# A decoder layer on one core: attention scores as one float32r product of high and low parts, strips spread in one transfer per half, maxima split and used on the chip

## The chip, the cores and the metric

The kernel runs on one core of a Trainium2 chip. The core has five engines with instruction streams of their own: TensorE (PE, with its weight loads shown as PEld), VectorE (DVE), ScalarE (ACT), GpSimd (POOL) and SyncE (SP), which here issues every DMA. The metric is the time of one execution on the device in microseconds, the median of the runs.

## What is computed

The reference is one decoder layer on 32 batches of 256 positions with 256 features. Three parts follow each other, each with a residual and a layer norm: a selective scan (state space) block, a cross attention with 16 heads of width 16, and a gated feed-forward net with 8 experts. The part that the change touches is the attention, shown here without the projections of q, k and v:

```python
scores = jnp.einsum('bhqd,bhkd->bhqk', q, k) / np.sqrt(D_K)   # 16 heads, D_K = 16
attn = jax.nn.softmax(scores, axis=-1)
out = jnp.einsum('bhqk,bhkd->bhqd', attn, v)
x = _layernorm(x + (out.transpose(0, 2, 1, 3).reshape(B, S, D_MODEL) @ w_o.T + b_o))
# before it: the scan block; after it: 8 experts, each on its own 32 positions
h_t = dA_t * h_{t-1} + dBu_t ;  y_t = sum_n h_t * C_t          # the scan, 512 x 16 states
out = (silu(x @ w1[e]) * (x @ w3[e])) @ w2[e]                  # an expert unit
```

## The kernel before

**Order of the work.** The kernel is a set of generators, each a chain of steps: `decays`, `scan`, `weighted`, `sums` for the scan block, `pres` and `steps` for its projections, `keys_ahead`, `keys`, `queries`, `maxima`, `attns`, `finishes` for the attention, `units` and `seconds` for the expert units. When the program is built, `in_order` picks the next step by a planned clock for each engine: `spend` adds a planned cost (`MM`, `EV`, `VE`, `CV`, `GP`, `LANDING`) and a chain says when its next step can start. So the instructions of an engine stand in one fixed order, written when the program is built, and each engine runs its own list in that order. A step that waits holds everything behind it in the same list. All DMAs stand in the list of SP.

**The scan.** There are 32 x 16 = 512 scan steps. A step loads a strip `ld` (two DMAs of 256 KB, `load_step`, three steps ahead), ACT makes `da` (L573), DVE multiplies `bu` (L602) and scans `h` (L621), POOL multiplies `h` by `c_bc` (L637), and after four steps TensorE sums `y` (L651). There are six `h` buffers.

**The attention before.** `keys_ahead` makes k for every batch, feature by position: a float32 product (L349), an ACT copy with the bias into `k_flat`, one DMA into `k_all` in the device's memory. `queries` does the same with q, into `heads`. `spread_heads` (L678) then reads them back so that each head has 16 of the 64 rows of a strip: for each half (8 heads) two DMAs for `kT` and two for `qT`. `qT` waits for `scored` of the batch before, which still uses the strip.

`scores` (L809) multiplies two heads at a time, one in rows 0 to 63 and one in rows 64 to 127 of the array, each in two tiles of 128 positions: four float32 products of 64 (or 63) x 128 by 64 x 256. `maxima` (L825) calls it with q on the left, 4 times for each half, and DVE takes the maximum over the keys (L838). TensorE transposes the maxima (L844), ACT negates them into `rows` (L847), one DMA writes them to the device's memory (`tops`) and another reads them back into row 63 of each strip of `qT`. Row 63 of `kT` holds ones there, so that `attns` (L874), which calls `scores` with k on the left and all 64 rows, gets scores with the maxima already subtracted. ACT takes the exponential (L894), TensorE multiplies by v (L863), and `finish` transposes, divides, projects (`ps_o`) and stores x2d.

**The experts.** 32 expert units need the x2d of eight batches each, or of four for the last eight units. The last four need batch 31. A unit loads weights and inputs, has products `ps_h` (L1133) for w1 and w3 and `ps_down` (L1212) for w2.

**PSUM.** The two-dimensional products share a ring of five banks (`ps_mm`), which `take` and `done` hand out.

Of the kernel before, what the change touches and what calls it, by code (L numbers as in the profile page):

```python
# [7 lines left out]

F32 = mybir.dt.float32
AF = mybir.ActivationFunctionType  # L10
ALU = mybir.AluOpType
AX = mybir.AxisListType
# [3 lines left out]
P = 128  # L16
B, L, D = 32, 256, 256
# [5 lines left out]
NQ = NS // NL  # L23
GB = 2
# [73 lines left out]
def decoder_kernel(ctx: ExitStack, tc: tile.TileContext, a: dict, out: bass.AP):  # L98
# [18 lines left out]

    k_all = dram.tile([B, D, L], F32, name="k_all")
    v_all = dram.tile([B, L, D], F32, name="v_all")
# [45 lines left out]

    def heads(n):

        w = wp.tile([P, 2, D], F32, tag="w_" + n, name="w_" + n)
        src = a["w_" + n].rearrange("(k p) (h c) -> p k h c", p=P, c=32)
        for k in range(2):  # L170
            dst = w[:, k].rearrange("p (h c) -> p h c", c=DK)
            dma(dst, src[:, k, :, :DK])
        bias = wp.tile([P, 2], F32, name="b_" + n)
        for g in range(NG):
            r = 64 * (g % 2)
            src = a["b_" + n].rearrange("(j c) g -> j c g", c=32)[:, :DK, g : g + 1]
            dma(bias[r : r + 64, g // 2 : g // 2 + 1], src)
        return w, bias
# [29 lines left out]

    later = []
    now, dma = dma, lambda dst, src: later.append((dst, src))  # L210
    w_k, b_k = heads("k")
    w_v = weight("w_v", D, D)
    b_out = row("b_out")
    w_out = weight("w_out", DI, D)
    w_q, b_q = heads("q")
    w_o = weight("w_o", D, D)
# [53 lines left out]

    kT = keep.tile([P, HG, L], F32, name="kT")
    last = small.tile([P, 1], F32, tag="ln_st", name="last")
    at = ident.rearrange("p (j c) -> p j c", c=HR)[:, :, HR - 1]
    nc.vector.tensor_reduce(last, at, AX.X, ALU.add)
    nc.vector.tensor_copy(kT.rearrange("p g t -> p (g t)"), last.to_broadcast([P, HG * L]))
    qT = keep.tile([P, HG, L], F32, name="qT")
    nc.gpsimd.memset(qT, 0.0)

# [27 lines left out]

    MM = 0.47
    EV = {1: 0.47, 2: 0.6, 4: 1.06}
    VE = {1: 0.41, 2: 0.69, 4: 1.23}
    CV = 0.565  # L310
    GP = {1: 0.7, 2: 1.27, 4: 2.36}

    def layernorm(tiles, t):

        n = len(tiles)
        mv = small.tile([P, n, 2], F32, tag="ln_mv", name="ln_mv")
        for i, x in enumerate(tiles):
            st = small.tile([P, 6], F32, tag="ln_st", name="ln_st")
            nc.vector.bn_stats(st, x)
            nc.vector.bn_aggr(mv[:, i, :], st)  # L320
        yield spend("DVE", 0.6 * n, t), "POOL"
        rstd = small.tile([P, n, 1], F32, tag="ln_rstd", name="ln_rstd")
        nc.gpsimd.tensor_scalar_add(rstd, mv[:, :, 1:2], EPS)  # L323
        nc.gpsimd.tensor_tensor(rstd, rstd, power[:, :n, :], ALU.pow)
        off = small.tile([P, n, 1], F32, tag="ln_off", name="ln_off")
        nc.gpsimd.tensor_tensor(off, mv[:, :, 0:1], rstd, ALU.mult)
        nc.gpsimd.tensor_scalar_mul(off, off, -1.0)
        yield spend("POOL", 1.5), "ACT"
        for i, x in enumerate(tiles):
            nc.scalar.activation(  # L330
                x, x, AF.Identity, bias=off[:, i, :], scale=rstd[:, i, :]
            )
        return spend("ACT", 0.6 * n)

# [29 lines left out]
    def rest():  # L364

        while later:
            yield 0.0, "SP"
            dma(*later.pop(0))

    xps, dds, sress, bcds, ygs, us, spread, silus = {}, {}, {}, {}, {}, {}, {}, []  # L370
# [175 lines left out]
    def decays():  # L546
# [15 lines left out]
        for i in range(STEPS):  # L562
# [8 lines left out]
            for g in range(GB):  # L571
                for q in range(NQ):
# [5 lines left out]
                    )  # L578
            decayed[i] = spend("ACT", GB * NQ * 0.5)

    read = {-1: 0.0}

    def scan():
# [4 lines left out]
        for i in range(STEPS):  # L588
# [39 lines left out]
            )  # L628
            recurred[i] = spend("DVE", 2.29)
            read[i] = max(multiplied, decayed[i])  # L630
# [45 lines left out]
    scored = {}  # L676

    def spread_heads(b, dst, d, t, there):  # L678

        yield t, "SP"  # L680
        for half in range(2):
            if b:
                yield lambda: max(t, scored[b - 1, half]) if (b - 1, half) in scored else None, "SP"
            for j in range(2):
                src = d.rearrange("(i g j c) t -> i j c g t", i=2, j=2, c=DK)[half, j]
                dma(dst[HR * j : HR * j + DK, 4 * half : 4 * half + 4, :], src)
            there[b, half] = clock.at["SP"] + LANDING
# [3 lines left out]
    def keys_ahead():  # L691

        for b in range(B):
# [14 lines left out]
            done(1, tk)  # L708
            yield tk, "SP"
            dma(k_all[b].rearrange("(m p) t -> p m t", p=P), flat)  # L710
            yield from take(1, rank, t0)
# [77 lines left out]
    def queries():  # L789
        for b in range(B):  # L790
# [12 lines left out]
            done(1, tq)  # L803
            yield tq, "SP"
            d = bcd.tile([D, L], F32, tag="heads", name="heads")
            dma(d.rearrange("(m p) t -> p m t", p=P), flat)
            yield from spread_heads(b, qT, d, clock.at["SP"] + LANDING, qts)

    def scores(heads, left, right, n):  # L809


        ss = [bank("s").rearrange("p (t n) -> p t n", t=2) for _ in heads]
        for t in range(2):
            for h, s in zip(heads, ss):
                g, r = h // 2, HR * (h % 2)
                nc.tensor.matmul(  # L816
                    s[:, t, :],
                    left[r : r + n, g, t * P : (t + 1) * P],
                    right[r : r + n, g, :],
                    start=True,  # L820
                    stop=True,
                )
        return ss, spend("PE", 2 * MM + 0.2)

    def maxima():  # L825

        for i in range(2 * B):
# [5 lines left out]
            while h < 8:  # L833
                yield from take(2, 2, t0)
                ss, ts = scores(range(8 * half + h, 8 * half + h + 2), qT, kT, HR - 1)
                for s in ss:
# [3 lines left out]
                    done(1, t)  # L840
                    h += 1
            yield from take(1, 1, t)
            ps = bank("ps_m")[:H, :P]
            nc.tensor.transpose(ps, top.rearrange("p j g t -> p (j g t)"), ident)  # L844
            yield spend("PE", 0.2), "ACT"
            rows = unit2.tile([H, P], F32, tag="rows", name="rows")
            nc.scalar.activation(rows, ps, AF.Identity, scale=-1.0)  # L847
            t = spend("ACT", 0.35)
            done(1, t)
            yield t, "SP"  # L850
            d = bcd.tile([2, 4 * L], F32, tag="tops", name="tops")
            dma(d.rearrange("j (i n) -> (j i) n", n=P), rows)
            yield clock.at["SP"] + LANDING, "SP"
            dst = qT[HR - 1 :: HR, 4 * half : 4 * half + 4]
            dma(dst.rearrange("j g t -> j (g t)"), d)
            tts[b, half] = clock.at["SP"] + LANDING

# [16 lines left out]
    def attns():  # L874

        for n in range(2 * B):
# [4 lines left out]
            for g in range(3):  # L881
                ess = []
                while g < 2 and len(ess) < 4:
                    yield from take(2, 2, tq)
                    h = 8 * half + 4 * g + len(ess)
                    ss, ts = scores(range(h, h + 2), kT, qT, HR)
                    if g and not ess:
# [454 lines left out]
```

## Time and profile before

| | |
|---|---|
| median of 3 runs | 2742.55 us (2738.98 to 2750.74) |
| profiled execution | 2743.78 us, span 2742.0 us |
| PE busy | 2466.3 us, 90% of the span |
| DVE busy | 2380.6 us, 87% |
| ACT busy | 2043.4 us, 75% |
| POOL busy | 1643.7 us, 60% |
| granted TensorE clock, mean | 0.959 |
| DMA | 505.86 MB, the main queue 64.8% of 16 engines |

The span runs from the first to the last instruction. Busy time is the union of an engine's instructions. A float32 product appears as two records, so 1024 products of `scores` for the maxima are 2048 records. The profile's slices show DVE at nine tenths or more until the last tenth of the span, where it falls to one to two tenths and TensorE goes on.

### The profile page before, as it was taken

How to read it: one execution, taken by the hardware profiler on the slowest of the kernel's cores; microseconds unless marked ns; L12 is line 12 of the kernel's file. 1: busy time of each engine (PE TensorE's matmuls, PEld its weight loads, DVE VectorE, ACT ScalarE, POOL GpSimd, SP SyncE). 2: the span in 40 equal slices, each digit the busy share in tenths (PEclk: the TensorE clock that was granted, in tenths of full speed). 3: DMA queues.
4: the chain of work that ended last, by engine and by line, in shares of the span. 5: the costliest groups of instructions: out<-in, count | busy, mean ns of one | idle time of the engine just before them, and what ended most of it. 6: DMA issues, size and time to landing. Idle time of an engine off the chain costs nothing.

```text
span 2742.0 us, 48659 instructions
## 1 busy us (share of the span) xinstructions
PE 2466.3 (90%) x16964; PEld 1705.3 (62%) x16964; DVE 2380.6 (87%) x2413; ACT 2043.4 (75%) x4327; POOL 1643.7 (60%) x1145
## 2 busy tenths in 40 slices
PE   5788989889899899989998989999999899998988
PEld 4565666566566666666666666665666566666767
DVE  4999999999999999999999999999999899896212
ACT  6887888888778878887878778888788788674331
POOL 4775766666666666575666665666666666553000
PEclk8899999999999999998999999999999999999999
DMA  7866666666676666676666666667666566666464
GB/s 203 228 199 176 193 187 181 189 191 191 187 199 186 181 167 190 176 197 177 167 198 187 198 175 186 187 177 195 190 197 179 163 172 180 185 174 181 150 195 144
DMA packets 491497, 505.86 MB, mean 184 GB/s; under 512 B 177204, under 2 KB 339252, under 8 KB 491252
## 3 DMA queue, kind: packets, MB, share of 16 engines
q1 hardware_dynamic: 491252, 502.75, 64.8%
q8 instruction: 135, 2.21, 0.4%
q14 instruction: 110, 0.90, 0.1%
HBM read 426.07 MB, written 76.55 MB: 183 GB/s over the span
## 4 chain that ended last, share of the span: by engine, by line
PE 29%; DVE 11%; ACT 8%; DMA 5%; issue 3%; POOL 1%; SPq 1%; DVEq 0%; ACTq 0%; POOLq 0%
PE ps_h L1133 8%; PE s L816 6%; DVE h L621 5%; PE ps_down L1212 4%; ACT da L573 3%; PE y L651 3%; DVE bu L602 2%; DVE tops L838 2%; PE ps_in L349 2%; PE ps_oT L863 2%; DMA ld<-dd 1%; DMA xe<-x2d 1%; PE ps_out L349 1%; PE ps_qk L349 1%; ACT es L894 1%
## 5 line engine op out<-in xcount | busy, mean ns | idle before, releaser
L637 POOL TENSOR_TENSOR h<-h,c_bc 128x1024 f32<-128x1024 f32 x512 | 1209.1, 2362 | 740.6 <-DVE h L621 627.0
L621 DVE TENSOR_TENSOR_SCAN h<-da,bu 128x1024 f32<-128x1024 f32 x512 | 1168.9, 2283 | 50.4 <-ACT da L573 5.8
L573 ACT ACTIVATE da<-ld,a_neg 128x252 f32<-128x252 f32 x2048 | 864.6, 504 | 188.3 <-DVE h L621 138.4
L602 DVE TENSOR_TENSOR bu<-ld,b_bc 128x1024 f32<-128x1024 f32 x512 | 626.1, 1223 | 19.9 <-DMA ld<-dd 8.0
L816 PE MATMUL s<-kT,qT 63*128 63x256 f32 x2048 | 345.4, 416 | 45.6 <-DVE tops L838 22.8
L894 ACT ACTIVATE es<-s 128x512 f32<-128x512 f32 x512 | 277.9, 594 | 140.6 <-PE s L816 75.9
L838 DVE TENSOR_REDUCE tops<-s 128x2 f32<-128x512 f32 x512 | 325.2, 677 | 41.6 <-PE s L816 41.1
L1133 PE MATMUL ps_h<-x2T,w 128*128 128x256 f32 (+2 forms) x1536 | 343.5, 368 | 9.5 <-ACT es L894 1.7
L816 PE MATMUL s<-qT,kT 64*128 64x256 f32 x2048 | 313.8, 405 | 22.5 <-DMA qT<-tops 13.0
L651 PE MATMUL y<-h,sel_y 128*32 128x256 f32 x4096 | 280.8, 397 | 52.3 <-POOL h L637 36.9
L816 PEld LDWEIGHTS s<-kT,qT 63*128 63x128 f32 x2048 | 213.8, 193 | 151.9 <-DVE tops L838 50.8
L1133 PEld LDWEIGHTS ps_h<-x2T,w 128*128 128x128 f32 (+1 forms) x1536 | 246.7, 186 | 89.7 <-issue 35.1
L349 PE MATMUL ps_in<-xT,w_in 128*128 128x256 f32 x1024 | 258.4, 397 | 8.7 <-ACT da L573 2.6
L816 PEld LDWEIGHTS s<-qT,kT 64*128 64x128 f32 x2048 | 200.9, 189 | 102.3 <-issue 39.6
L651 PEld LDWEIGHTS y<-h,sel_y 128*32 128x32 f32 x4096 | 131.8, 113 | 177.4 <-POOL h L637 55.1
L349 PEld LDWEIGHTS ps_in<-xT,w_in 128*128 128x128 f32 x1024 | 192.8, 196 | 60.4 <-issue 12.9
L420 POOL TENSOR_TENSOR u<-u,shifted 128x512 f32<-128x512 f32 x128 | 151.4, 1183 | 39.7 <-ACT u L407 34.7
L323 POOL TENSOR_SCALAR ln_rstd<-ln_mv 128x2 f32<-128x2 f32 x96 | 20.9, 218 | 254.2 <-DVE ln_mv L320 250.0
L407 ACT ACTIVATE shifted<-ps_in,tap_b,conv_w 128x256 f32<-128x256 f32 x256 | 130.8, 567 | 22.5 <-PE ps_in L349 10.9
L863 PE MATMUL ps_oT<-es,v 128*32 128x256 f32 x2048 | 142.4, 391 | 3.7 <-DVE h L1197 1.2
L349 PE MATMUL ps_out<-w_out,yg 128*128 128x256 f32 x512 | 117.6, 383 | 0.4 <-DVE yg L667 0.4
L375 ACT ACT_TABLE_LOAD x90 | 115.5, 1283 | 1.4
(135 smaller groups left out, 2987.5 us busy)
## 6 DMA issues: line engine op xcount, KB each, us to landing
ld<-dd SPq DMA_DIRECT2D x1024, 256.0 KB
w<-in_w SPq DMA_DIRECT2D x128, 352.0 KB
x<-in_x SPq DMA_DIRECT2D x64, 256.0 KB
dd<-delta SPq DMA_DIRECT2D x32, 512.0 KB
dd<-u SPq DMA_DIRECT2D x32, 512.0 KB
w<-in_w SPq DMA_DIRECT2D x32, 384.0 KB
w13y<-in_w SPq DMA_DIRECT2D x32, 352.0 KB
c_bc<-bcd SPq DMA_DIRECT2D x64, 128.0 KB
```

Of the source, the lines that this page charges most:

```text
L349: nc.tensor.matmul(ps[:, j, :], l, r, start=(k == 0), stop=(k == len(terms) - 1))
L420: nc.gpsimd.tensor_tensor(u[:, cc], u[:, cc], at, ALU.add)
L573: nc.scalar.activation(da[:, g, q].rearrange("p (k t) -> p k t", t=CHUNK)[:, :, 1:], loads[i][:, 0, g].rearrange("p (k t) -> p k t", t=CHU ...
L602: nc.vector.tensor_tensor(bu, loads[i][:, 1].unsqueeze(2).to_broadcast([P, GB, NQ, L]), b_bc.unsqueeze(1).to_broadcast([P, GB, NQ, L]), AL ...
L621: nc.vector.tensor_tensor_scan(h.rearrange("p g q t -> p (g q t)"), das_of.pop(i).rearrange("p g q t -> p (g q t)"), bu.rearrange("p g q t ...
L637: nc.gpsimd.tensor_tensor(hs[i], hs[i], c_bc, ALU.mult)
L651: nc.tensor.matmul(y[32 * j : 32 * j + 32, :], sel_y[:, g, :], hs[i - NJ + 1 + j][:, g, q, :], start=(g == 0 and q == 0), stop=(g == GB - ...
L816: nc.tensor.matmul(s[:, t, :], left[r : r + n, g, t * P : (t + 1) * P], right[r : r + n, g, :], start=True, stop=True,)
L838: nc.vector.tensor_reduce(top[:, h % 2, h // 2, :], s, AX.X, ALU.max)
L863: nc.tensor.matmul(oT[32 * j : 32 * j + 32, :], v[:, k, 4 * g + j, :], ess[j][:, k, :], start=(k == 0), stop=(k == 1), tile_position=(0, 3 ...
L894: nc.scalar.activation(es, s, AF.Exp, scale=1.0 / DK**0.5)
L1133: nc.tensor.matmul(ps[:m, i, :], w_tiles[u, which, e][k][:, f * P : f * P + m], right, start=(k == 0), stop=(k == 1),)
```

## The change

- **High and low parts.** After the bias, POOL copies q or k to a float32r tile (`hi`), and subtracts it from the full value into `lo`, which takes the place of the flat tile. `k_all` gets three parts (hi, lo, hi), `heads` gets two (hi, lo). The features are ordered by column position first, so that one half of the heads lies in one block of 128 rows. The weights `w_k` and `w_q` are reordered once by POOL at the start, and their biases come in eight small DMAs each instead of four.
- **Strips.** All 64 rows of a strip are filled by one transfer of 64 rows x 4 KB instead of 16 rows of 4 x 1 KB: In blocks of 16 rows `kT` holds hi, lo, lo, hi and `qT` holds hi, lo, hi, lo. One float32r product over 64 rows then adds all four products of the parts.
- **Scores.** `scores` uses float32r operands and all 64 rows. For `attns` each product is followed by a second one, `pick` (a column with ones at the head's two rows, high and low, spread over 128 columns) times `mTs`, which adds the negated maximum in the same PSUM bank.
- **Maxima.** POOL splits the maxima of a half into `padded` (high, low), TensorE transposes two blocks of 128x128, ACT negates them into `mTs`. The two DMAs through `tops`, and row 63 as a place for them, are gone.
- **Planned costs.** Several constants of the planner are different (`MM`, `EV`, `VE`, `CV`, `GP`, the costs of `decays`, `scan`, `layernorm`), so every list is ordered anew.

```diff
+    def parts_of(n, b, full, t, d):
+        hi = unit1.tile([P, 2, L], F32R, tag="hi", name=f"{n}_hi_{b}")
+        lo = full.bitcast(F32R)
+        yield t, "POOL"
+        nc.gpsimd.tensor_copy(hi, full)
+        nc.gpsimd.tensor_tensor(lo, full, hi.bitcast(F32), ALU.subtract)
+        t = spend("POOL", 2 * GP[2])
+        yield t, "SP"
+        for s, part in enumerate((hi, lo, hi)[: d.shape[1]]):
+            dma(d[:, s].rearrange("i p t -> p i t"), part.bitcast(F32))
...
     def spread_heads(b, dst, d, t, there):
...
             for j in range(2):
-                src = d.rearrange("(i g j c) t -> i j c g t", i=2, j=2, c=DK)[half, j]
-                dma(dst[HR * j : HR * j + DK, 4 * half : 4 * half + 4, :], src)
+                at = dst[HR * j : HR * (j + 1), NG * half : NG * (half + 1), :]
+                at = at.bitcast(F32).rearrange("p g t -> p (g t)")
+                src = d[half, 0, NG * j : NG * (j + 1)]
+                again = 0 if dst is qT else P * L
+                rows = [[again, 2], [2 * NG * L, 2 * DK], [1, NG * L]]
+                dma(at, bass.AP(src.tensor, src.offset, rows))
...
-            yield tk, "SP"
-            dma(k_all[b].rearrange("(m p) t -> p m t", p=P), flat)
+            yield from parts_of("k", b, flat, tk, k_all[b])
...
-            yield tq, "SP"
-            d = bcd.tile([D, L], F32, tag="heads", name="heads")
-            dma(d.rearrange("(m p) t -> p m t", p=P), flat)
+            d = bcd.tile([2, 2, P, L], F32, tag="heads", name="heads")
+            yield from parts_of("q", b, flat, tq, d)
...
-    def scores(heads, left, right, n):
+    def scores(heads, left, right, lowered):
...
-                    left[r : r + n, g, t * P : (t + 1) * P],
-                    right[r : r + n, g, :],
+                    left[r : r + HR, g, t * P : (t + 1) * P],
+                    right[r : r + HR, g, :],
                     start=True,
-                    stop=True,
+                    stop=not lowered,
                 )
+            for h, s in zip(heads, ss):
+                g, r = h // 2, HR * (h % 2)
+                if lowered:
+                    nc.tensor.matmul(
+                        s[:, t, :],
+                        pick[r : r + HR, g : g + 1].to_broadcast([HR, P]),
+                        mTs[g // NG][r : r + HR, :],
+                        start=False,
+                        stop=True,
+                    )
...
+            yield t, "POOL"
+            r = 2 * NG * half
+            hi, lo = padded[:, :, :, r : r + NG], padded[:, :, :, r + NG : r + 2 * NG]
+            full = top.rearrange("p j g t -> p t j g")
+            nc.gpsimd.tensor_copy(hi, full)
+            nc.gpsimd.tensor_tensor(lo, full, hi.bitcast(F32), ALU.subtract)
+            t = spend("POOL", 0.5)
             yield from take(1, 1, t)
-            ps = bank("ps_m")[:H, :P]
-            nc.tensor.transpose(ps, top.rearrange("p j g t -> p (j g t)"), ident)
-            yield spend("PE", 0.2), "ACT"
-            rows = unit2.tile([H, P], F32, tag="rows", name="rows")
-            nc.scalar.activation(rows, ps, AF.Identity, scale=-1.0)
...
-            dma(d.rearrange("j (i n) -> (j i) n", n=P), rows)
-            yield clock.at["SP"] + LANDING, "SP"
-            dst = qT[HR - 1 :: HR, 4 * half : 4 * half + 4]
-            dma(dst.rearrange("j g t -> j (g t)"), d)
+            ps = bank("ps_m")[:, :L]
+            for k in range(2):
+                src = padded[:, k].rearrange("p j r -> p (j r)").bitcast(F32)
+                nc.tensor.transpose(ps[:, k * P : (k + 1) * P], src, ident)
+            yield spend("PE", 0.6), "ACT"
+            nc.scalar.activation(mTs[half], ps, AF.Identity, scale=-1.0)
```

## The prediction

> **What bounds the kernel now.** I read the page first: VectorE is busy 87% of the span and TensorE 90%, but not in the same places. So the second view is a table of stretches, cut where the last of the 512 scan steps ends (2513.4 us). Columns: stretch, its length, then busy time with instructions of PE, PEld, DVE, ACT, POOL, then granted clock, DMA share, GB/s.
>
> ```profile
> 0.00:2513.40 2513.40, 2268.35 (x15567) 1545.11 (x15567) 2327.76 (x2294) 1972.37 (x4194) 1623.93 (x1095) 0.96 0.66 186
> 2513.40:2742.00 228.60, 198.00 (x1399) 160.22 (x1397) 52.85 (x119) 71.03 (x133) 19.76 (x50) 0.93 0.54 172
> ```
>
> Two stages, two limits. Up to the last scan DVE works 2327.8 of 2513.4 us; 37 us of its idle time lie in the first 60 us. The tail of 228.6 us is TensorE's. So the change can gain in the first stage only what DVE loses to others, and in the tail whatever it takes from TensorE's list. Third view, who made DVE wait between 60 and 2513 us (total, times, longest):
>
> ```profile
> DVE tops L838 <- PE s L816: 22.5, 26, 3.5
> DVE yg L667 <- PE y L651: 16.1, 14, 3.0
> DVE xe L1224 <- PE ps_down L1212: 13.0, 4, 6.9
> DVE x L964 <- PE ps_o L349: 10.2, 9, 2.6
> ```
>
> All rows of that answer with PE as releaser add up to 78 us, those with ACT, POOL or DMA to about 10; the other 60 us of idle time are short gaps between neighbours (bu ends, the scan starts 0.13 us later). So 78 us is what a faster TensorE can give back there.
>
> **Scores on TensorE.** Fourth view, the timeline of PE, start and length of merged pieces; the distance between two starts is the price.
>
> ```profile
> 1016.63 1.14 PE L816 MATMUL s<-qT,kT 64*128 64x256 f32 x8
> 1017.70 0.66 PE L935 MATMUL ps_oB<-ident,oS 128*128 128x128 f32 x4
> ...
> 1031.06 1.05 PE L863 MATMUL ps_oT<-es,v 128*32 128x256 f32 x16
> 1032.03 1.99 PE L1133 MATMUL ps_h<-x2T,w 128*128 128x256 f32 x8
> ```
>
> One call of scores() is four float32 products, shown as 8 records, and takes 1.07 us: 133 ns a record. 512 calls take 548 us (the groups show 659 busy, since ends overlap waits). No float32r product is in this trace. Upper bound: it costs what a float32 one does, two records, 265 ns. Lower bound: the cheapest 256-column record of the trace, 61 ns (0.97 us for the 16 of ps_oT, four side by side). I take one record instead of two, 133 ns, the row of the same shape and row groups. A call for maxima keeps four products: 0.53 us. A call for attention gets four more, pick times mTs: 1.06 us, no gain. Sum 256 x (0.53 + 1.06) = 407 us, so 141 us less; with 61 ns 187 us, 361 us less; with 265 ns 814 us, 266 us more. The transpose of the maxima becomes two products of 128x128 (the 4 of ps_oB take 0.53 us, so 0.13 each): 64 x 0.13 = 8 us more.
>
> The Trainium skill (TensorE: Matmul & The Clock Gate, sections "Back-to-back issue gap" and "LDWEIGHTS") gives N/2.4 + 2.5 ns for a pass, 109 ns at 256 columns, and P/1.2 for a weight load whatever the rows, 107 ns at 128 columns. That speaks against the pick products, which load 128 columns of weights to subtract one row of maxima: by it a call is bound by its loads, 0.43 us for maxima and 0.85 us for attention, and the sum would be 328 us. The load records of L816 here last 182 to 190 ns, longer than the page's 107, but most lie beside a product.
>
> **What of that reaches the scan.** I price each product in PE's instruction list (256 columns 0.456 us, 128 columns 0.237, ps_oT 0.122, y 0.111, transposes 0.135, scores as above). Up to the last y product the old list holds 2086 us of work in 2518 us, the new one 1995. TensorE isn't full there; it is late at single moments, in order, behind other products. With a shorter list I let half of the 78 us go: -39 us. Both ends stay: 0 and -78.
>
> **DVE** has the same 2413 instructions. In its new order 24 expert units end before the last scan instead of 23 (4.3 us each), and the last two reductions of batch 30 stand before it: +6 us before the last scan.
>
> **POOL** gets, for k and for q of each batch, a copy and a subtraction of 128x512. The nearest row is L420, 1183 ns: 64 x 2.37 = 152 us. For the maxima of each half two operations on 32 elements; L323 and L326 show 218 and 195 ns: 64 x 0.42 = 27 us. POOL goes from 1644 to about 1823 us. It has 741 us of idle time before its products h, 627 of them waiting for the scan, so time is there, but it runs in order: a pair of 2.4 us ahead of a product h holds the y products and the six h buffers.
>
> **SP.** The change takes away 128 small DMAs and their waits, from the waits of the DMA queue:
>
> ```profile
> SPq L105 <- ACT rows L847: 62.8, 33, 6.9
> SPq L105 <- DMA tops<-rows: 39.5, 18, 4.5
> ```
>
> 102 us in which everything behind them stood, the ld loads of the scan too. In their place the first write of k or q waits for POOL, 64 times, and behind it stand the same ld loads. Before, those writes waited 3.9 and 3.8 us in all on ACT. Bounds: from below zero (102 us of waits gone) to 64 x 2.4 = 154 us. SP's waits reach the scan weakly: ACT waited 31.9 us for ld in this stretch, DVE 1.3 us for ld and 5.8 us for da. I take +10 us for POOL and SP together. The cover is the load three steps ahead (about 14 us at 4.8 us a step); if that cover is gone, the 154 us count in full.
>
> **DMA bytes.** Strips: 256 transfers of 256 KB instead of 64 KB, +50.3 MB; k_all in three parts, +16.8; heads in two, +8.4; tops gone, -1.0. That is 74.5 MB on 502.75 MB at 64.8%, so about 74% of the engines. I cost it at nothing while the load three steps ahead covers a strip (two transfers of 256 KB; 502.75 MB at 64.8% of 2742 us is 283 GB/s, so 1.85 us); without that cover it is 64 x 1.85 = 119 us for each of kT and qT. ACT evacuates 128x256 instead of 16x128: oS shows 375 ns, k_flat 476, rows 259, so 64 x 0.12 to 0.22 = 7 to 14 us, hidden at 75% load.
>
> **Start.** Eight more small bias DMAs stand in SP ahead of bcd and the first ld (b_k: 2.34 us for 4), and POOL reorders w_k and w_q ahead of batch 1's u. Some of that is hidden behind delta; I take +3 us (0 to 8).
>
> **Tail.** From the last y product (2518) to the last ps_o of batch 31 (2631) the old list holds 99.6 us of products in 113 us, the new one 76.5 us: fewer unit products (120 of 128 columns instead of 168), since more of them stand before the last scan. At the same ratio 87 us: -26. A chain is also cut out there; view: the chain that ended last, start and length.
>
> ```profile
> 2528.07 8.26 DMA tops<-rows
> 2536.43 4.64 DMA qT<-tops
> 2541.11 2.08 PE s L816 x8
> ```
>
> Against its 12.9 us stand POOL's 2.4 us on q and the larger heads write. I leave that in the ratio. After ps_o of batch 31 the four units that need it follow, 111 us in both.
>
> **Sum.** 2742.0 - 39 + 6 + 10 + 3 - 26 = 2696 us of span. The profiled run took 2743.78, 1.8 above its span, and the median of the runs lies 1.2 below it: 2697.
>
> **Rivals.** (a) The gain in the first stage is zero, because the waits of DVE come from the order and not from the length of PE's list: 2742 + 6 + 10 + 3 - 26 = 2735. For it: TensorE's list fills only 83% of the stretch. Against: the chain that ended last runs through PE for 29% of the span and through DVE for 11%, and many of its PE pieces lie before 2500. (b) Slower, one mechanism: the wait of SP for POOL's subtraction. POOL stands in order behind products h that wait for the scan, SP behind POOL, ld behind SP. Half of 154 us passed on, with the relief gone: 2742 + 77 + 6 + 3 - 26 = 2802; all of it 2879. The forecast has 46 us in hand, so it decides from 0.7 us per pair. For it: POOL waited 627 us for the scan. Against: the 102 us of SP waits that go. (c) float32r products cost what float32 ones do: the new list up to the last y is then 2388 us, and at the old 83% the stretch takes 2880, so some 3100. Then the change doesn't do what it says. (d) 61 ns a record, all 78 us gone, POOL and start hidden: 2742 - 78 + 6 - 30 = 2640.
>
> **How the numbers follow.** Forecast 0.58 (2660 to 2728), (a) 0.17, (b) 0.15, (c) 0.05, (d) 0.05. Range 2640 to 2790: it leaves out half of (b), (c) and half of (d), under 0.2. About 0.5% is what a measurement of this kernel can tell from no change, so faster means below 2729: the forecast, (d) and a quarter of (a), 0.67. Slower means above 2756: (b), (c) and a little of (a), 0.22. The rest 0.11.
>
> **What would show it.** Right: scores for maxima near 0.5 us a call, for attention near 1; DVE's waits on PE before the last scan near 40 us; the last scan near 2494; last y to last ps_o near 87 us. Wrong: SP waiting on k_hi or q_hi for over 100 us, DVE waiting on ld or da for over 30, products h in long POOL queues, or a call of scores above 1.5 us.

## The result and the profile after

The changed kernel took 3814.55 us (median of 4 runs, 3803.67 to 3820.96) against 2743.94 us for the kernel before on the same chip: ratio 1.3895 [1.3851, 1.394]. The forecast was 2697, the range ended at 2790. The profiled execution took 3820.96 us, 1.7 us above its span.

The page of the changed kernel, busy time of each engine, the main DMA queue (packets, MB, share of 16 engines), then the shares of the chain that ended last; the second block has those shares in the kernel before:

```profile
span 3819.3 us, 47065 instructions
PE 2546.7 (67%) x16004; PEld 1763.5 (46%) x16004; DVE 2399.1 (63%) x2413; ACT 2058.7 (54%) x4331; POOL 1786.5 (47%) x1409
q1 hardware_dynamic: 511700, 577.19, 53.0%
...
DMA 35%; PE 18%; ACT 8%; DVE 7%; SPq 6%; issue 4%; POOL 2%; ACTq 0%; DVEq 0%; POOLq 0%
```
```profile
PE 29%; DVE 11%; ACT 8%; DMA 5%; issue 3%; POOL 1%; SPq 1%; DVEq 0%; ACTq 0%; POOLq 0%
```

DVE works about as long as before (2399 us against 2381), in a span that is 1077 us longer. No engine is full, the DMA engines have fewer bytes per us than before (152 GB/s, 184 before), and yet the chain runs through DMA for 35% of the span (5% before). The stretches, cut at the last scan (columns as in the prediction):

```profile
0.00:3588.67 3588.67, 2379.02 (x14879) 1626.17 (x14880) 2352.25 (x2307) 2002.45 (x4227) 1765.32 (x1357) 0.79 0.54 152
3588.67:3819.30 230.63, 167.66 (x1126) 137.37 (x1124) 46.88 (x106) 56.23 (x104) 21.17 (x52) 0.87 0.49 152
```

Everything was lost ahead of the last scan: 2513.4 became 3588.7. Who waited for whom (total us, times, longest), in the changed kernel and, in the second block, in the kernel before:

```profile
ACT da L600 <- DMA ld<-dd: 999.6, 129, 29.9
DVE tops L888 <- PE s L856: 605.9, 120, 22.3
PE s L856 <- DMA qT<-heads: 340.9, 57, 17.8
DVE yg L694 <- PE y L678: 169.9, 52, 11.1
DVE bu L629 <- DMA ld<-dd: 89.8, 34, 18.8
```
```profile
ACT da L573 <- DMA ld<-dd: 44.4, 17, 6.0
PE s L816 <- DMA qT<-heads: 5.9, 3, 4.1
DVE bu L602 <- DMA ld<-dd: 8.0, 3, 6.3
```

ACT waits for the scan's own loads a thousand us (44.4 before), TensorE for the strips, and DVE for TensorE. Two pieces of the chain (start, length), and SP's queue in the same stretch:

```profile
2035.88 22.37 DMA qT<-heads
2097.62 16.52 DMA ld<-dd
```
```profile
2034.75 2.14 SPq L106 DMA_DIRECT2D qT<-heads  x4
2036.93 14.94 SPq L106 DMA_DIRECT2D w<-in_w  x4
2051.97 2.96 SPq L106 DMA_DIRECT2D ld<-dd  x2
```

Four strips are issued in 2.14 us, and the chain follows them for 22.37 us until they have landed. That is 1 MB, which takes 3.7 us at the rate of 283 GB/s that the prediction used. What is issued behind them stands: the four w loads take SP 14.94 us to hand out, and the next ld is issued 17 us after the strips.

The packet records of the trace show why. A strip is 64 packets of 4 KB, each in flight for 162 ns in the median. During 88% of the time in which such packets are in flight there are exactly two of them, and a pair of strips (128 packets) takes 12 to 14 us. All packets of the main queue together stand at exactly two for 29% of the span (2.2% before). 64 x 0.162 / 2 = 5.2 us for one strip, 4 x 5.2 = 21 us for the four above.

The same records show how ld is held up. In the first piece only 4 KB packets, two at a time, are in flight from 2037 to 2047 us (apart from three of 4 bytes); the first packet of the w loads starts at 2047.3, though SP began with them at 2036.93. In the second piece two kT strips (issued at 2096.38) are in flight until 2113.0. Four ld transfers follow them at 2097.62, 512 packets of 2 KB: 448 of these, 14 of 16, have landed by 2104.5. After that 112 of the 128 of the next ld transfer (issued at 2107.57) land by 2110.3, and the rest of these transfers starts only at 2112, as the strips come to their end. The chain's ld lands at 2114.1. So two sixteenths of these ld transfers waited behind the strips.

**Theories.** E: the strip's source pattern, `[[again, 2], [2*NG*L, 2*DK], [1, NG*L]]`, has a first dimension of 2, and a transfer is dealt to only so many DMA engines; those two then hold up every transfer dealt over all of them, ld first. The records show packets and not engines: that the two packets at a time are two engines is an inference from the two sixteenths above and from the next paragraph. Rivals: the bytes themselves (the 64-row strips and the extra writes); POOL's steps with SP behind them (the prediction's rival b); a bad order of the lists.

The Trainium skill (DMA: Bandwidth & Descriptors, section "Rules for kernel authors") states E as a rule: a transfer whose outermost dimension has a size c below 16 uses at most c engines, and a leading broadcast of c copies is its example. The two packets at a time agree with it, and so do the four of the first experiment.

### The profile page after: what moved, and what is told of

The parts are those of the page before. It is cut to its first block, busy times and chain, and to the rows that moved or that the text cites. A ratio compares the mean times of both kernels' runs of the same rounds, so it can differ in the third digit from the quotient of the medians.

```text
span 3819.3 us, 47065 instructions
## 1 busy us (share of the span) xinstructions
PE 2546.7 (67%) x16004; PEld 1763.5 (46%) x16004; DVE 2399.1 (63%) x2413; ACT 2058.7 (54%) x4331; POOL 1786.5 (47%) x1409
## 4 chain that ended last, share of the span: by engine, by line
DMA 35%; PE 18%; ACT 8%; DVE 7%; SPq 6%; issue 4%; POOL 2%; ACTq 0%; DVEq 0%; POOLq 0%
DMA ld<-dd 19%; SPq L106 6%; DMA qT<-heads 5%; PE ps_h L1185 4%; ACT da L600 4%; DVE h L648 3%; DMA x2d<-x 3%; PE ps_down L1264 3%; PE s L856 2%; DMA x<-in_x 2%; PE ps_oT L915 2%; DVE bu L629 2%; DVE tops L888 2%; PE y L678 2%; DMA xe<-x2d 1%
## 5 line engine op out<-in xcount | busy, mean ns | idle before, releaser
L629 DVE TENSOR_TENSOR bu<-ld,b_bc 128x1024 f32<-128x1024 f32 x512 | 626.4, 1223 | 121.5 <-DMA ld<-dd 89.8
L856 PE MATMUL s<-kT,qT 64*128 64x256 f32 x1024 | 202.7, 404 | 463.1 <-DMA qT<-heads 340.9
L1185 PE MATMUL ps_h<-x2T,w 128*128 128x256 f32 (+3 forms) x1632 | 405.9, 399 | 35.0 <-ACT x2T L1173 21.4
L856 PEld LDWEIGHTS s<-kT,qT 64*128 64x128 f32 x1024 | 127.2, 237 | 559.6 <-issue 408.5
L372 PE MATMUL ps_in<-xT,w_in 128*128 128x256 f32 x1024 | 315.9, 464 | 51.3 <-ACT xT L412 30.3
L1185 PEld LDWEIGHTS ps_h<-x2T,w 128*128 128x128 f32 (+1 forms) x1632 | 290.9, 209 | 122.3 <-issue 30.2
L856 PE MATMUL s<-qT,kT 64*128 64x256 f32 x1024 | 207.9, 357 | 139.3 <-ACT es L946 99.0
L856 PEld LDWEIGHTS s<-qT,kT 64*128 64x128 f32 x1024 | 137.6, 217 | 213.6 <-ACT es L946 113.5
L866 PE MATMUL s<-mT,pick 64*128 64x256 f32 x1024 | 177.1, 322 | 4.2 <-ACT mT L905 4.2
L372 PE MATMUL ps_o<-w_o,aT 128*128 128x256 f32 x256 | 94.6, 533 | 116.0 <-ACT aT L1006 115.8
L801 POOL TENSOR_TENSOR x<-x,b_out 128x512 f32<-128x512 f32 x32 | 40.6, 1267 | 270.1 <-DMA x<-in_x 194.3
```

The lines of the kernel that those rows point to most:

```text
L372: nc.tensor.matmul(ps[:, j, :], l, r, start=(k == 0), stop=(k == len(terms) - 1))
L629: nc.vector.tensor_tensor(bu, loads[i][:, 1].unsqueeze(2).to_broadcast([P, GB, NQ, L]), b_bc.unsqueeze(1).to_broadcast([P, GB, NQ, L]), AL ...
L856: nc.tensor.matmul(s[:, t, :], left[r : r + HR, g, t * P : (t + 1) * P], right[r : r + HR, g, :], start=True, stop=not lowered,)
L1185: nc.tensor.matmul(ps[:m, i, :], w_tiles[u, which, e][k][:, f * P : f * P + m], right, start=(k == 0), stop=(k == 1),)
```

## The experiments

### The pattern of the strips

The strips of the change in two transfers of 32 rows, with a first dimension of 4:

```diff
-                rows = [[again, 2], [2 * NG * L, 2 * DK], [1, NG * L]]
-                dma(at, bass.AP(src.tensor, src.offset, rows))
+                rows = [[2 * NG * L, 4], [8 * NG * L, DK // 2], [1, NG * L]]
+                for n in range(2):
+                    part = at[2 * DK * n : 2 * DK * (n + 1)]
+                    dma(part, bass.AP(src.tensor, src.offset + n * again, rows))
```

> The changed kernel with each strip transfer cut in two of 32 rows, each with a first dimension of 4 (every fourth row, then 8 of them). A dose between 2 and 32. Theory E: four engines carry 8 packets of 162 ns each per transfer, 1.3 us, two such transfers a strip, so half of the 5.2 us; 4 KB packets mostly four to eight at a time; the excess over the version with 32 first should be clearly there but well under half: 2800 to 3250 us. Rival B (bytes) and rival P (SP behind POOL): the same 3700 to 3850 us. If the number of transfers matters (256 more on SP at about 0.5 us), somewhat longer than that in each case.

Measured: 3126.89 us, ratio 1.1394 [1.1376, 1.1412]. Four 4 KB packets are in flight during 76% of the time in which there are any, and a pair of strips takes 7 to 8 us instead of 12 to 14. SP has 256 more transfers to issue, so the order of the lists is new.

One transfer, with the two outer dimensions exchanged, so that the first has 32 steps. Nothing else: the list of every engine is the same, instruction for instruction, as in the change (row 2c + s of a strip, s up to 1 and c up to 31, now holds what row 32s + c held, in k and q alike).

```diff
-                rows = [[again, 2], [2 * NG * L, 2 * DK], [1, NG * L]]
+                rows = [[2 * NG * L, 2 * DK], [again, 2], [1, NG * L]]
```

> The changed kernel with one edit: the source pattern of a strip transfer names its 32 rows first and the repetition of 2 second, instead of the repetition first. Same number of transfers, same bytes, same 64 packets of 4 KB, same values in kT and qT up to one common order of rows. Theory E (engines): a transfer is dealt out over the DMA engines along the first dimension of its pattern; with 2 there only two engines carry 64 packets of 162 ns, 5.2 us a transfer, and whatever has packets behind them on these two engines, the ld loads above all, is late. In the trace of the changed kernel exactly two packets are in flight for 29% of the time (2% before), and 4 KB packets are two at a time for 88% of their time. E expects the strips to spread like other loads, ACT's wait for ld to fall from 1000 us to under 80 us, and a time of 2680 to 2780 us. Rival B (bytes): 74.5 MB more in rows of 4 KB are too much beside ld; nothing of that changes, so 3700 to 3850 us. Rival P (the wait that my prediction priced as its slower case): SP stands behind POOL's subtraction and ld behind SP; nothing of that changes either, 3700 us or more.

Measured: 2830.32 us, ratio 1.0325 [1.0294, 1.0356]. 984 us are gone by one line that moves the same bytes. A pair of strips now takes 3 to 4 us, with 13 to 17 packets at once during half of that. So the first dimension of the pattern is shown as the cause of these 984 us, neither bytes nor POOL nor the order. But the kernel is still slower than before, and above the 2680 to 2780 us that were expected with E alone, so E is not all. The page, the stretches and the waits of this kernel:

```profile
PE 2362.0 (83%) x16004; PEld 1649.3 (58%) x16004; DVE 2383.0 (84%) x2413; ACT 2065.3 (73%) x4331; POOL 1787.7 (63%) x1409
q1 hardware_dynamic: 515284, 577.20, 74.4%
```
```profile
0.00:2625.67 2625.67, 2199.45 (x14885) 1516.11 (x14886) 2336.17 (x2307) 2009.14 (x4227) 1766.58 (x1357) 0.89 0.76 208
2625.67:2829.70 204.03, 162.59 (x1120) 133.22 (x1119) 46.86 (x106) 56.14 (x104) 21.11 (x52) 0.90 0.56 171
```
```profile
DVE tops L888 <- PE s L856: 117.3, 64, 15.3
ACT da L600 <- DMA ld<-dd: 85.3, 42, 8.2
PE s L856 <- DMA qT<-heads: 55.9, 33, 7.1
```

Against the kernel before, the tail is 24.6 us shorter (228.6 then), and the stretch up to the last scan 112 us longer. All DVE waits on PE until the last scan add up to 179 us (78 before).

The same strips in two transfers of 32 rows each, first dimension 32:

```diff
+                rows = [[2 * NG * L, 2 * DK], [1, NG * L]]
+                for n in range(2):
+                    part = at[2 * DK * n : 2 * DK * (n + 1)]
+                    dma(part, bass.AP(src.tensor, src.offset + n * again, rows))
```

> The changed kernel with each strip transfer cut in two of 32 rows, first dimension 32. Theory E: within 2% of the version with one transfer and 32 first, 2680 to 2800 us; the 256 more DMA issues at about 0.5 us each are 128 us on SP, spread over the span. Rivals B and P: 3700 to 3850 us.

Measured: 2866.52 us, ratio 1.0449 [1.0425, 1.0473]: 36 us more with 256 more transfers in SP's list. The order is new too, and what each of the two costs was not separated.

### The bytes

All kernels of this part start from the one with 32 outer steps. First, only the high parts are written and read; the low parts are left out of the scores.

```diff
-        for s, part in enumerate((hi, lo, hi)[: d.shape[1]]):
+        for s, part in enumerate((hi,)):
...
-                at = dst[HR * j : HR * (j + 1), NG * half : NG * (half + 1), :]
+                at = dst[HR * j : HR * j + DK, NG * half : NG * (half + 1), :]
...
-                rows = [[2 * NG * L, 2 * DK], [again, 2], [1, NG * L]]
+                rows = [[2 * NG * L, DK], [1, NG * L]]
```

> The strip pattern with 32 outer steps, and only the high parts written and read: the strips are again 16 rows (64 KB), the DMA bytes those of the kernel before less tops. POOL still computes the low parts, PE has the same products; what is left out are the low parts in the scores. Theory B (the wide strips and their writes are what is left of the loss, 2830 against 2744): about 2700, with qT ahead of the scores under 15 us of PE's waits (56 in the kernel with 32 steps). Theory O (the new order, with POOL's steps in it): 2800 to 2830.

Measured: 2759.36 us, ratio 1.0051 [1.0035, 1.0067]. 71 of the 86 us above the kernel before are gone with the bytes, in a new order of the lists; the gain over the kernel before that was expected (about 2700) does not come.

All parts written again, but strips of 16 rows read (only the first line of that diff undone):

> The kernel with only high parts in the strips (2759), but all five parts written to the device's memory as in the change (25 MB more). It tells writes from reads in the 71 us between it and the kernel with 32 outer steps (75 MB more). By bytes alone a third: 2780 to 2785. If the wide strips (four times as many rows per strip, and scores waiting for them) are the cost: 2759 to 2770.

Measured: 2774.82 us, ratio 1.0114 [1.0092, 1.0136], between the two ranges expected, and again in another order than the kernel with high parts only.

From there, the 64-row strips for kT alone, then for qT alone (here the rows of k and q no longer pair, so the scores are others):

```diff
+                wide = dst is kT
+                at = dst[HR * j : HR * j + (HR if wide else DK), ...]
...
+                if wide:
+                    rows = [[2 * NG * L, 2 * DK], [P * L, 2], [1, NG * L]]
```

> As the kernel that writes all five parts and reads 16-row strips (2775), but the strips of kT are read in full (64 rows, 256 KB); those of qT stay at 16 rows. Half of the 50 MB that separate it from the kernel with 32 outer steps (2830). If the cost goes by bytes: 2795 to 2810. If it is the time from q to its scores, which kT's strips do not lengthen: 2775 to 2785.

> The mirror image: the strips of qT are read in full, those of kT stay at 16 rows. If by bytes: 2795 to 2810, as the other. If it is the time from q to its scores: 2815 to 2830.

Measured: kT wide 2799.73 us, ratio 1.0195 [1.0179, 1.0212]; qT wide 2818.67 us, ratio 1.028 [1.025, 1.031]. Neither expectation alone holds for both. kT's wide strips cost 25 us, as the bytes would have it, and qT's 44 for the same bytes. The 19 us between them fit that q is read back right after it was written, while its scores wait: TensorE waits for qT 27.8 us with no wide strip, 34.8 with kT's and 49.2 with qT's. Together they cost 55 us, less than 25 + 44. These four kernels and the change have the same order of instructions on every engine (two fills at the start apart), so the steps between them (2775, 2800, 2819, 2830, 3815) are the strips' alone. Along this row the mean granted clock is 0.902, 0.898, 0.899, 0.895 and 0.795, and DVE's waits on PE until the last scan grow as the time does: 122, 145, 163, 179 and 1025 us.

POOL's subtraction taken out of the kernel with high parts only:

```diff
         nc.gpsimd.tensor_copy(hi, full)
-        nc.gpsimd.tensor_tensor(lo, full, hi.bitcast(F32), ALU.subtract)
-        t = spend("POOL", 2 * GP[2])
+        t = spend("POOL", GP[2])
```

> The kernel with only high parts in the strips (2759), without POOL's subtraction (64 of 1.27 us, 81 us less on POOL; the low parts are left out anyway). If POOL's steps are what is left of the loss against the kernel before: 2740 to 2750. If they are hidden: 2755 to 2765.

Measured: 2761.97 us, ratio 1.006 [1.0041, 1.0079]: the same as with it. POOL is busy 78 us less and no gain is seen; the planner knows of it, so the order differs here too.

### The order

The kernel with 32 outer steps, its planner told of later landings:

```diff
-            there[b, half] = clock.at["SP"] + LANDING
+            there[b, half] = clock.at["SP"] + 2.5 * LANDING
...
-            yield from spread_heads(b, qT, d, clock.at["SP"] + LANDING, qts)
+            yield from spread_heads(b, qT, d, clock.at["SP"] + 1.5 * LANDING, qts)
```

> The strip pattern with 32 outer steps, and the planner told that a heads write takes 1.5 times and a strip 2.5 times LANDING, so products wait in the list behind other work until the strips are there. Nothing else. Theory O (the order puts scores where their strips have not landed, and everything on PE stands behind them): 2740 to 2780, DVE waiting for scores at tops under 50 us (117). Theory B (the bytes themselves): 2820 to 2840, since later scores only move the wait.

Measured: 2815.71 us, ratio 1.0259 [1.0241, 1.0277]. TensorE's wait for the strips falls from 55.9 to 6.3 us and DVE's for the scores from 117.3 to 71.6, yet only 15 us come back, and neither expectation is met: ACT's wait for ld rises from 85.3 to 138.2.

The same kernel with the planned costs of before:

```diff
-    MM = 0.49
+    MM = 0.47
...
-            recurred[i] = spend("DVE", 2.285)
+            recurred[i] = spend("DVE", 2.29)
```

> The strip pattern with 32 outer steps, and the planned costs MM, EV, VE, CV, GP, those of decays, scan and layernorm as in the kernel before. If the new planned costs made the order worse: 2740 to 2800. If not: 2820 to 2845.

Measured: 2866.6 us, ratio 1.0444 [1.0427, 1.0462]. That lies above both expectations: with the old costs the order is 36 us worse here. The mirror image, the kernel before with the new costs:

> The kernel before with the changed kernel's planned costs (MM, EV, VE, CV, GP, those of decays, scan and layernorm) and nothing else: only the order of each engine's list differs. The old constants in the kernel with 32 outer steps cost 36 us (2867 against 2830). If the new ones are better in themselves: 2700 to 2730. If they only fit the changed kernel: 2740 to 2760.

Measured: 2745.21 us, ratio 0.9998 [0.9979, 1.0018]. There the new costs are worth nothing. So what they do to the time depends on the kernel that they order.

### TensorE's list and the maxima

The kernel before, with float32r products for the maxima alone:

```diff
-    kT = keep.tile([P, HG, L], F32, name="kT")
+    kT = keep.tile([P, HG, L], F32R, name="kT")
...
-                    ss, ts = scores(range(h, h + 2), kT, qT, HR)
+                    ss, ts = scores(range(h, h + 2), kT.bitcast(F32), qT.bitcast(F32), HR)
...
-        return ss, spend("PE", 2 * MM + 0.2)
+        return ss, spend("PE", 2 * MM + 0.2 if n == HR else 0.45)
```

The last line tells the planner of the lower price, so the lists are ordered anew here as well.

> The kernel before with one edit: the scores of the maxima are float32r products of the same strips (a maximum that is a little off cancels in the softmax); attention keeps float32. No byte, no POOL step and no wait is added; 256 calls fall from 1.07 to 0.43 to 0.53 us, 140 to 160 us less on PE. If PE's length is what DVE waits for (the prediction's first term): 2690 to 2710. If the waits come from the order (its rival a): 2730 to 2745.

Measured: 2744.92 us, ratio 1.0006 [0.9988, 1.0024]. Its page, its stretches, its waits between 60 and 2513 us, and in the last block the second of these waits in the kernel before:

```profile
PE 2379.1 (87%) x15940; PEld 1639.6 (60%) x15940; DVE 2384.0 (87%) x2413; ACT 2048.7 (75%) x4329; POOL 1644.2 (60%) x1145
```
```profile
0.00:2521.84 2521.84, 2205.11 (x14770) 1500.26 (x14771) 2336.53 (x2305) 1989.47 (x4218) 1625.79 (x1099) 0.93 0.67 187
2521.84:2735.30 213.46, 174.02 (x1173) 139.31 (x1171) 47.45 (x108) 59.27 (x111) 18.44 (x46) 0.91 0.50 157
```
```profile
DVE tops L839 <- PE s L817: 34.9, 35, 3.0
...
PE s L817 <- DVE tops L839: 62.5, 65, 3.5
```
```profile
PE s L816 <- DVE tops L838: 25.4, 29, 3.0
```

PE is busy 87 us less, and the last scan ends 8 us later. DVE's waits on PE add up to 75.0 us (78 before). The rows on `tops` say who sets the pace there: TensorE now waits 62.5 us for DVE to take scores out of the banks (25.4 before), and DVE 34.9 us for scores (22.5 before). This kernel's timeline of DVE shows the two reductions of one call:

```profile
1006.60 1.28 DVE L839 TENSOR_REDUCE tops<-s 128x2 f32<-128x512 f32 x2
```

1.28 us, and between one such pair and the next stand scans and products of DVE's list. The pairs took 1.25 to 1.29 us in the kernel before too, against 1.07 us for a call of float32 products: the slower side of this exchange was DVE already. And the granted clock is 0.927 instead of 0.959, with 405 ns instead of 397 for a y record and 381 instead of 368 for a ps_h record, in the mean.

The same with the new planned costs:

> The kernel before with float32r products for the maxima (2745) and with the new planned costs (2745 alone). It is the base of the kernel that uses the maxima on the chip (2754). If the new costs together with shorter maxima make the order worse: 2752 to 2760. If the 10 us come from using the maxima on the chip: 2738 to 2748.

Measured: 2772.14 us, ratio 1.0095 [1.0068, 1.0122], above both ranges.

The maxima used on the chip, without the wide strips: the kernel with float32r maxima, the new costs, and from the change `padded`, `pick`, `mTs` and the second products; attention's first products stay float32.

```diff
+        f = lambda x: x.bitcast(F32) if lowered else x
...
+                    f(left)[r : r + HR, g, t * P : (t + 1) * P],
+                    f(right)[r : r + HR, g, :],
...
+        return ss, spend("PE", 1.45 if lowered else 0.45)
```

> The strips, writes and attention products of the kernel before (float32, 16 rows), float32r products for the maxima, the maxima split, transposed and used on the chip by the pick products, and the new planned costs. No wide strip, no split of q and k, no DMA through tops. PE's list is some 40 to 50 us shorter than before (maxima 140 to 160 less, pick 256 times 0.43 more, transposes 8 more). If the 102 us of SP's waits for the maxima mattered: 2700 to 2730. If neither they nor PE's length are what DVE waits for: as the kernel before with the new planned costs, within 10 us.

Measured: 2754.49 us, ratio 1.0038 [1.0017, 1.0058]. The round trip through memory, with its 102 us of SP waits, is gone, and the time is no better than before. DVE's waits on PE are 107 us. The same with attention planned 7 us later (`tts[b, half] = t + 2 * LANDING`):

> As the kernel with float32 attention and maxima used on the chip (2754), but the planner lets attention start 7 us later, as it did when the maxima went through two DMAs. If attention, planned straight behind the maxima, crowds TensorE's list and keeps y and ps_h behind it: 2735 to 2747, DVE's waits on PE back to 75 to 90 (107). If the chain itself costs: 2752 to 2765.

Measured: 2769.97 us, ratio 1.008 [1.005, 1.0109], above both ranges. Attention at once again, but with the maxima reduced straight into `padded`:

```diff
-                    nc.vector.tensor_reduce(top[:, h % 2, h // 2, :], s, AX.X, ALU.max)
+                    at = 2 * NG * half + h // 2
+                    nc.vector.tensor_reduce(padded[half][:, :, h % 2, at], s, AX.X, ALU.max)
```

> As the kernel with float32 attention and maxima used on the chip (2754), but DVE's reductions write straight into the padded tile (float32r, one for each half, no low part: the maximum cancels in the softmax), so no POOL step stands between the maxima and TensorE. If POOL's step in the chain of the maxima is why DVE waits 107 us for PE there, against 75 in the kernel with float32r maxima alone: 2725 to 2740, DVE's waits on PE 75 to 85. If the chain through the transposes and PE's order costs it all the same: 2750 to 2760.

Measured: 2767.52 us, ratio 1.0079 [1.0063, 1.0095], above both ranges, with 110 us of DVE waits on PE. Without POOL's step the waits did not come down. Both forms once more, with the old planned costs:

> Float32 attention, float32r maxima used on the chip, and the planned costs of the kernel before. With the new costs this use on the chip is 18 us faster than the same without it (2754 against 2772). If that is a property of the step: 2745 minus 18, so 2720 to 2735, faster than both kernels. If 15 to 30 us either way are only what a new order does: anything from 2730 to 2775.

> The same with DVE's reductions written straight into the padded tile, no POOL step and no low part of the maxima; with the new costs it was 13 us slower than the form with POOL's step (2767 against 2754), which has no reason in its instructions. If the order made that: within 15 us of e19 on either side. If the step itself: 10 to 15 us above e19.

Measured: 2762.27 us, ratio 1.0063 [1.0041, 1.0084], and 2757.03 us, ratio 1.0037 [1.0022, 1.0052]. With the new costs the direct form was 13 us slower, with the old ones it is 5 us faster. The 18 us that use on the chip seemed to gain (2772 to 2754) turn into a loss of 17 (2745 to 2762). So differences of this size can't be put down to these steps: the order that each edit happened to get explains them as well. No kernel tried here beats the one before.

## Why the prediction was wrong, step by step

**DMA bytes: the step that failed.** The prediction costed 74.5 MB at nothing, "while the load three steps ahead covers a strip", and took 1.85 us for two strips from the mean rate of the whole queue. That rate is one of transfers spread over many engines; this pattern's strips ran two packets at a time. A pair took 12 to 14 us, the cover of about 14 us was used up by the strips alone, and the bound of 119 us "without that cover" used the same rate: 238 us for both at the most. The pattern stood in the diff. The sign that the prediction named, DVE waiting on ld for over 30 us, came: 89.8. The size: 984 us (change against 32 outer steps, same order). Of the 1118 us between forecast and result, 71 more went with the bytes, in a new order, and 62 lie between the forecast and the 2759 us that are left without both.

**The same term, mended, isn't nothing either.** Reading the wide strips costs 55 us at the same order. With the extra writes the time is 15 us higher, but there the order differs too. The prediction's bounds, 0 to 119 for each of kT and qT, held this; its choice of 0 did not.

**Stage one, -39 us.** It didn't come. With the maxima at less than half price, in the order that this gives, PE is busy 87 us less and DVE's waits on PE are 75 us instead of 78. The step took the waits as a share of the length of PE's list, and that share failed. In its place the runs show that DVE is the slower side of the exchange of the maxima, and that the clock was lower. That the other waits come from single moments of the order fits this, but was not shown apart, since the order changed with the price. The prediction's rival (a) expected no gain in this stage; it gave 2735, and the kernel with the pattern mended and the low parts left out stands at 2759.

**Score prices.** Too high, on the safe side. The timeline of PE in the changed kernel, a call for maxima and what follows it, then a call for attention and what follows it:

```profile
2062.77 0.50 PE L856 MATMUL s<-kT,qT 64*128 64x256 f32 x4
2063.20 1.99 PE L372 MATMUL ps_in<-xT,w_in 128*128 128x256 f32 x8
```
```profile
2105.49 0.38 PE L856 MATMUL s<-qT,kT 64*128 64x256 f32 x2
2105.71 0.28 PE L866 MATMUL s<-mT,pick 64*128 64x256 f32 x2
2105.82 0.28 PE L856 MATMUL s<-qT,kT 64*128 64x256 f32 x2
2105.94 0.28 PE L866 MATMUL s<-mT,pick 64*128 64x256 f32 x2
2106.15 1.99 PE L1185 MATMUL ps_h<-x2T,w 128*128 128x256 f32 x8
```

From the first start to the start of the next product it is 0.43 us for maxima (0.53 predicted) and 0.66 us for attention (1.06 predicted). In the kernel with 32 outer steps the median attention call takes 0.67 us.

By the page of the Trainium skill that the prediction cites (TensorE: Matmul & The Clock Gate, sections "Back-to-back issue gap" and "LDWEIGHTS") the estimates were 0.43 and 0.85 us; for attention they differ from the measurement, and the measurement decides. The 0.43 agrees by luck: the page's pass of 109 ns is no shorter than its load of 107, so "bound by its loads" did not follow. The records of these two kernels show another build-up. The two products of a pair, one in each half of the array, start 4 ns apart in the median; pairs inside an attention call start 0.11 to 0.12 us apart, and at the first pair and behind the last one stand some 0.2 us. So pick's two pairs add about 0.23 us to a call. With the measured prices the sum is 256 x (0.43 + 0.67) = 282 us, not 407: TensorE got more room than the sum gave it, and no gain came of it.

**POOL and SP.** POOL's pair costs 0.61 + 1.27 = 1.88 us (2.37 predicted), POOL 1786.5 us (1823). SP waited 39.3 us for POOL's parts in the changed kernel, not over 100: rival (b) did not happen, and the kernel without the subtraction is no faster. But from the relief set against it, 102 us of SP's waits, no gain was seen either.

**Start and tail** were right: the first scan begins 2.4 to 4.4 us later (3 predicted), and the tail is 24.6 us shorter where the strips are mended (26 predicted). The reason given holds there too: from the last y product to the last ps_o it is 91.9 us (87 predicted, 113 before), with 240 records of ps_h between them instead of 336. In the changed kernel itself the tail is 2.0 us longer.

**What stays open.** Pairs of kernels that differ in planned costs or landings alone lie 36, 27, 15, 15, 10, 8 and 0 us apart. A difference of that size between two kernels with different orders can't be put down to a step of the edit; that holds for the 14 us between the kernel before and the one with high parts only. Seven of these kernels (2759, 2816, 2867, 2775, 2768, 2772 and 2770 us) lay in none of the ranges expected for them: what a new order does was not forecast well. How much of TensorE's saving the lower clock takes back was not separated from the order.

## What to carry to other kernels

Before a transfer is costed by its bytes, look at the first dimension of its pattern: with 2, 4 and 32 the same bytes gave 3815, 3127 and 2830 us here. A slow transfer on a few engines delays the transfers behind it that are spread over all: here each ld waited for its last two sixteenths. A shorter list on an engine can give time back only at the moments when another engine waits for it: read which side of each exchange is the slower one (here two reductions of 1.28 us against a call of 1.07) before counting a share of the waits. And where a planner orders everything anew, measure how far the time moves when only its constants change, before a few tens of us are explained.

## What the runs showed of the hardware

- Transfers of 4 KB packets with a first dimension of 2 and 4 ran with exactly two and four packets at once in 88% and 76% of their time, with 32 in half of it with 13 to 17: a pair of 256 KB strips took 12 to 14, 7 to 8, and 3 to 4 us. In the median a 4 KB packet took 162 ns with a first dimension of 2 or 4, and 267 ns with 32.
- Behind two such strips 448 of 512 ld packets landed within 7 us of their issue, and the last 64, two sixteenths, started only as the strips came to their end, 14.4 us after it.
- The mean granted clock was lower where TensorE was busy a smaller share of the span: 0.959 at 90%, 0.927 at 87%, 0.895 at 83%, 0.795 at 67%. The Trainium skill (TensorE: Matmul & The Clock Gate, "Part 1: The HAM clock gate") says that the gate goes by how busy the array has been recently; these four profiles agree. TensorE's other work was slower with it: y records took 397, 405, 416 and 427 ns in the mean.
- Float32r products of 64 rows, side by side in the two halves of the array, started in pairs, 4 ns apart, a pair every 0.11 to 0.12 us inside a call. A call of eight took 0.67 us to the next product, one of eight float32 records (four products) 1.07 us.
